# Router rows of 4 in 26 edge columns picked by one-hot products in place of gathers, and each expert's weights asked for one expert ahead

## The chip, the core and the metric

The kernel runs on one core of one Trainium2 chip. The core has five engines, each with its own queue of instructions that it works through in order: TensorE (PE: matmuls; its weight loads are a row of their own, PEld), VectorE (DVE), ScalarE (ACT), GpSimd (POOL) and SyncE (SP, which here does nothing but issue DMAs). They wait for one another through semaphores. Sixteen DMA engines move data between DRAM and the on-chip memory SBUF; matmuls write to a second on-chip memory, PSUM. A gather by a list of row numbers (an indirect DMA) is issued from POOL, one instruction for 128 rows; plain DMAs are issued from SP.

The metric is the device time of one execution in microseconds, as a median over runs. Lower is better.

## The reference, cut to what matters

The model has a graph network over 103,125 edges, a linear-attention transformer of depth 4 beside it, and then a mixture of four experts whose router is itself a graph attention over 65,536 edges. The change lies in this last part. The reference of the router and the experts, with nodes x (3,125 rows of 256):

```python
h = (x_flat @ W_gat).reshape(M, HEADS, NUM_EXPERTS)
src = jnp.concatenate([edge_index[0], loops])
dst = jnp.concatenate([edge_index[1], loops])
a_src = (h * att_src).sum(-1)
a_dst = (h * att_dst).sum(-1)
e = leaky_relu(a_src[src] + a_dst[dst], negative_slope=0.2)
e_max = segment_max(e, dst, num_segments=M)
ee = jnp.exp(e - e_max[dst])
denom = segment_sum(ee, dst, num_segments=M)
alpha = ee / (denom[dst] + 1e-16)
msg = h[src] * alpha[:, :, None]
agg = segment_sum(msg, dst, num_segments=M).reshape(M, HEADS * NUM_EXPERTS) + b_gat
scores = layernorm(agg, ln_gamma, ln_beta).reshape(M, HEADS, NUM_EXPERTS).mean(1)
topk_s, topk_i = jax.lax.top_k(scores, TOP_K)
w = jax.nn.softmax(topk_s, axis=-1)
for ei in range(NUM_EXPERTS):
    g = jnp.where(topk_i == ei, w, 0.0).sum(-1)
    hh = gelu(x @ W1[ei] + b1[ei])
    out = out + g[..., None] * (hh @ W2[ei] + b2[ei])
```

What has to be fetched per edge is the source node's row: 16 values of h and 4 of a_src. The experts' products do not depend on the router; only the weights g with which they are added at the end do.

## The kernel before

**What comes first.** Up to about 1,900 us the kernel does the graph network and the transformer and, beside them, sorts the router's edges by their target node. The sort ends in a table in DRAM, `by_dst`, which holds the source node of each edge in sorted order; `sorted_edges` (L925) reads it back as the tile `si`, 128 partitions by 512 columns of node numbers. Only the first FEW = 400 columns hold edges here; columns from 400 on are worked only when a flag, `many`, is set (L1410), which it is not with these inputs. `finish` (L832) makes for every chunk of four node tiles the normed rows `hT`, the router's row of each node in `tab` (16 values of h, 4 of a_src, 4 of a_dst) and stores `tab` to DRAM as `tab_d` (L863).

**The stage of the change.** The 400 columns are cut into 16 chunks: 15 of 26 columns and a last one of 10 (`COLS`, L1247; `N_FEW` is 16).

- `gathered(j)` (L1255) takes one of three buffers `rows_c` and fills it for chunk j: one gather on POOL for each column, which fetches for 128 edges the rows of `tab_d` named by `si`.
- `edge_chunk(j, ...)` (L1272) works chunk j on DVE: it loads the targets' part `tg` from DRAM, adds source and target parts into `ev` (L1300, the first to read the rows), takes a running maximum by scans, and has ACT take two exponentials (`exp`, L1274, pinned to its place in ACT's order). It then multiplies the rows by the exponentials (L1315), runs 20 scans over them (L1321) and stores the chunk to DRAM (L1322). Each chunk carries on from the chunk before.
- `expert(e)` (L1342) is a generator: it loads an expert's weights (`we1`, `we2`, `be1`, each with a single buffer) and then yields seven pieces of work. A piece takes four tiles of 128 nodes (the last piece one): eight matmuls of 512 columns into three PSUM buffers `ps_a` (L1353), a Gelu on ACT for each of four results (L1355), then 16 matmuls of 256 columns and a bias product into `ps_t` (L1361, L1364) and a copy by ACT into `y_all` (L1367).

**The order.** The loop at L1382 sets it. For chunk j the program first asks for the gathers of chunk j + 1, then lays out the expert pieces up to (j + 1.5) x 1.75 of the 28, and then the edge chunk j. The last piece is kept for after the last chunk. The framework's planner may put an instruction ahead of earlier ones of its engine when those are not ready by its own reckoning; among ready ones the program's order counts. On the chip each engine's order is then fixed.

**What follows.** `fetch_sums` gathers 25 columns of finished sums, `over_partitions` joins the partitions' ends, `gates` makes the weights g, and `by_diagonals` and `by_turns` add up the experts' outputs and store the result.

**Buffers that the change borrows.** In the pool `so`, tiles with the same tag share a ring of buffers. The tags "hr" and "earlier" (two buffers each of 2 KB per partition), "oh_lo" (three), "oh_hi" and "run" (two), "pairs" and "place" (one each) belong to the edge sort, which is over when the stage begins; `si` itself sits in one of the "oh_hi" buffers. The tail uses "pairs" again for `sums`, "hr" for `more`, "earlier" for `ag` and `ag2`, and "oh_lo" for the small tiles of `across`.

Of the kernel before, what the change touches and what calls it, by code (L numbers as in the profile page):

```python
# [8 lines left out]
F32 = mybir.dt.float32  # L9
BF16 = mybir.dt.bfloat16  # L10
I32 = mybir.dt.int32
F16 = mybir.dt.float16
AF = mybir.ActivationFunctionType
ALU = mybir.AluOpType
AX = mybir.AxisListType
# [3 lines left out]
P = 128  # L19
N = 3125  # L20
NT = 25
NP = NT * P
LAST = N - (NT - 1) * P
D = 256
# [17 lines left out]
NEXP = 4  # L42
# [7 lines left out]
FEW = 400  # L50
NONE = NT * P - 1
FF2 = 512
# [7 lines left out]
def kernel(ctx: ExitStack, tc: tile.TileContext, a: dict, out: bass.AP):  # L60
    nc = tc.nc
    ctx.enter_context(nc.allow_non_contiguous_dma(reason="short vectors by partition"))
    V, S, G, T = nc.vector, nc.scalar, nc.gpsimd, nc.tensor
# [4 lines left out]
    dram = ctx.enter_context(tc.tile_pool(name="dram", bufs=1, space=DRAM))  # L68
    pg = ctx.enter_context(tc.tile_pool(name="pg", bufs=2, space=PSUM))
    pa = ctx.enter_context(tc.tile_pool(name="pa", bufs=3, space=PSUM))  # L70
    pt = ctx.enter_context(tc.tile_pool(name="pt", bufs=2, space=PSUM))
# [3 lines left out]
    ident = const.tile([P, P], F32, name="ident")  # L75
# [6 lines left out]
                    base=0, channel_multiplier=-1)  # L82
    after = const.tile([P, P], F32, name="after")
    G.affine_select(out=after, in_=ones, pattern=[[-1, P]], compare_op=ALU.is_gt, fill=0.0,
                    base=0, channel_multiplier=1)
# [45 lines left out]
    def by_column(pool, vec, c, name):  # L131
        t = pool.tile([P, c], F32, name=name)
        nc.sync.dma_start(t, vec.rearrange("(c p) -> p c", p=P))
        return t

    def weight(pool, w, c, n, name):
        t = pool.tile([P, c, n], F32, name=name)
        nc.sync.dma_start(t, w.rearrange("(c p) n -> p c n", p=P))
        return t
# [36 lines left out]
    hT = state.tile([P, 2, NP], F32, name="hT")  # L176
    tab = state.tile([P, NT, ROW + 1], F32, name="tab")
# [3 lines left out]
    so = ctx.enter_context(tc.tile_pool(name="so", bufs=1))  # L181
# [54 lines left out]
    ps = pg.tile([P, DM], F32, name="ps_g")  # L236
# [11 lines left out]
    e, e_src = (so.tile([P, TE], I32, name=f"e_{k}", tag="hr", bufs=2) for k in range(2))  # L248
# [95 lines left out]
    ps = pt.tile([P, 512], F32, name="ps_t")  # L344
# [11 lines left out]
    bin_p = const.tile([P, 1], F32, name="bin_p")  # L356
# [314 lines left out]
    place = so.tile([P, TE], I32, name="place")  # L671
# [259 lines left out]
    NCH = HG + H4  # L931
# [307 lines left out]
    ex = ctx.enter_context(tc.tile_pool(name="ex", bufs=1))  # L1239
# [3 lines left out]
    def gtile(shape, name, dt=F32, **k):  # L1243
        return ga_pool.tile(shape, dt, name=name, **k)

    CW = 28
    COLS = list(range(0, FEW, 26)) + list(range(FEW, TE, CW)) + [TE]  # L1247
# [4 lines left out]
    tgt_p = tgt_d[:E2, :].rearrange("(p t) h -> p t h", t=TE)  # L1252
    si = edges["si"]

    def gathered(j):  # L1255
        rows_c = gtile([P, CW, ROW], "rows_c", bufs=3)
        for t in range(COLS[j], COLS[j + 1]):
            G.indirect_dma_start(out=rows_c[:, t - COLS[j], :], out_offset=None, in_=tab_d,  # L1258
                                     in_offset=bass.IndirectOffsetOnAxis(ap=si[:, t:t + 1], axis=0))
        return rows_c  # L1260


# [70 lines left out]
    def y_of(e, t):  # L1333
# [5 lines left out]
            return hT[:, :, c0:c0 + P]  # L1339
        return hT[:, i // 2, c0 + i % 2 * D:c0 + i % 2 * D + D]  # L1340

    def expert(e):  # L1342
        we1 = weight(ex, a["L0_ffn_W1"][e], 2, FF2, "we1")
        we2 = weight(ex, a["L0_ffn_W2"][e], FF2 // P, D, "we2")
        be1 = by_column(ex, a["L0_ffn_b1"][e], FF2 // P, "be1")
        be2 = be2s[e]
        for c in FOURS:
            w = len(c) * P
            hh = []
            for f in range(FF2 // P):  # L1350
                ps = pa.tile([P, 512], F32, name="ps_a")
                for kc in range(2):
                    T.matmul(ps[:, :w], we1[:, kc, f * P:(f + 1) * P], hT[:, kc, c[0] * P:c[0] * P + w], start=kc == 0, stop=kc == 1)  # L1353
                hf = ex.tile([P, 512], F32, name="hf", bufs=5)
                S.activation(hf[:, :w], ps[:, :w], AF.Gelu, bias=be1[:, f:f + 1])  # L1355
                hh.append(hf)
            for i0 in range(0, len(c), 2):
                ts = c[i0:i0 + 2]
                k = len(ts)
                ps = pt.tile([P, 2, D], F32, name="ps_t")  # L1360
                T.matmul(ps[:, :k, :], ones_b, be2[:, :k, :], start=True, stop=False, skip_group_check=True)  # L1361
                for i in range(k):
                    for f in range(FF2 // P):
                        T.matmul(ps[:, i, :], hh[f][:, (i0 + i) * P:(i0 + i + 1) * P], we2[:, f, :],  # L1364
                                 start=False, stop=f == FF2 // P - 1, skip_group_check=True)
                if e < NEXP - 1:
                    S.copy(y_all[:, e, ts[0]:ts[-1] + 1, :], ps[:, :k, :])  # L1367
                elif k == 2:
                    S.copy(hT[:, i0 // 2, c[0] * P:c[0] * P + 2 * D], ps.rearrange("p t d -> p (t d)"))
                else:  # L1370
                    S.copy(hT[:, :, c[0] * P:c[0] * P + P], ps[:, 0, :].rearrange("p (a d) -> p a d", a=2))
            yield True

    be2s = [bias_rows(so, a["L0_ffn_b2"][e], f"be2{e}", tags) for e, tags in enumerate((
        ("own_bin", "lo", "base"), ("own_bin", "hi", "base"), ("own_bin", "ohT1", "base"), ("own_bin", "ohT0", "base")))]
    work = (w for e in range(NEXP) for w in expert(e))
    PIECES = NEXP * len(FOURS)
    EACH = PIECES / N_FEW
    done = 0
    last, taken = None, gathered(0)  # L1380
    many = nc.values_load(many_i[0:1, 0:1], min_val=0, max_val=1)
    for j in range(N_FEW):  # L1382
        rows_j = taken
        if j + 1 < N_FEW:
            taken = gathered(j + 1)

        while done < min((j + 1.5) * EACH, PIECES - 1) and next(work, False):
            done += 1
        last = edge_chunk(j, rows_j, last, j == N_FEW - 1)
        if j == 0:  # L1390
            V.tensor_scalar(flag0, flag0, -1.0, 1.0, op0=ALU.mult, op1=ALU.add)
            V.tensor_tensor(goes, f0[:, 0:1], f0[:, 1:2], op=ALU.is_equal)
            V.tensor_tensor(goes, goes, flag0[:, 1:2], op=ALU.mult)
            V.tensor_tensor(whole, goes, flag0[:, 0:1], op=ALU.mult)
            V.tensor_tensor(ends_in, flag0[:, 0:1], whole, op=ALU.subtract)
            V.tensor_scalar(whole_r, whole, -1.0, BIG, op0=ALU.add, op1=ALU.mult)
            V.tensor_scalar(own_row[:, 0:1], f0[:, 0:1], 0.0, float(NP - 1), op0=ALU.max, op1=ALU.min)
            V.tensor_single_scalar(own_row[:, 1:2], own_row[:, 0:1], 7, op=ALU.logical_shift_right)
            V.tensor_single_scalar(own_row[:, 0:1], own_row[:, 0:1], P - 1, op=ALU.bitwise_and)
            V.tensor_scalar(goes, bin_p, float(NP), None, op0=ALU.add)  # L1400
            V.scalar_tensor_tensor(flag0[:, 0:1], own_row[:, 0:1], float(NT), own_row[:, 1:2], op0=ALU.mult, op1=ALU.add)
            V.tensor_tensor(flag0[:, 0:1], flag0[:, 0:1], goes, op=ALU.subtract)
            V.scalar_tensor_tensor(carry_to, flag0[:, 0:1], ends_in, goes, op0=ALU.mult, op1=ALU.add)
            V.tensor_scalar(kept, ones, whole_r, None, op0=ALU.mult)
            ps = pg.tile([P, P], F32, name="ps_g")
            T.transpose(ps, kept, ident)
            V.tensor_copy(kept[:32, :], ps[:32, :])
    for _ in work:
        pass
    with tc.If(many > 0):  # L1410
        last = {"m": end_m, "ad": end_ad, "rows": end_rows}
        for j in range(N_FEW, len(COLS) - 1):
            last = edge_chunk(j, gathered(j), last, j == len(COLS) - 2)
# [193 lines left out]
    for _ in gates(1):  # L1607
        for _ in range(1):
            if len(laid_out) < 3:
                c = by_pe[len(laid_out)]  # L1610
                laid_out.append((c, by_diagonals(c)))
    n_laid = len(laid_out)
    for k, c in enumerate(by_pe):
        added(*laid_out[k])
        if n_laid < len(by_pe):
            c = by_pe[n_laid]
# [28 lines left out]
```

## Time and profile before

| what | value |
|---|---|
| median of 3 runs | 2523.63 us (2521.66 to 2525.22) |
| the profiled execution | 2525.02 us, span 2523.3 us |
| mean granted TensorE clock | 0.891 |
| PE busy | 1996.1 us (79% of the span) |
| DVE busy | 1397.8 us (55%) |
| ACT busy | 1169.1 us (46%) |
| POOL busy | 1791.2 us (71%) |
| first gather of `rows_c` issued | 1932.9 us |
| last gather of `rows_c` issued | 2441.6 us |
| in 1933 to 2443: PE, DVE, ACT, POOL busy | 367.3, 120.6, 142.3, 387.9 us |

How to read it: "busy" is the sum of an engine's instruction times as the hardware profiler recorded them; the time between two instructions is put down to whatever released the second ("issue" where nothing that the profile shows did). In the list of groups, a row gives source line, engine, operation, output and input tiles, count, then busy us and mean ns of one, then the idle time just before the group's instructions and what ended most of it. The slices cut the span into 40 equal parts of 63 us and give the busy share in tenths.

### The profile page before, as it was taken

Reading aid. Unit: us, or ns where it says so; the run is one execution under the profiler, and the core shown is the slowest. Engines: PE = TensorE matmul, PEld = TensorE weight load, DVE = VectorE, ACT = ScalarE, POOL = GpSimd, SP = SyncE. Lnnn points to the kernel's source line nnn. Section 1 sums busy time; section 2 is a strip of 40 time slices with the busy share of each in tenths; the row PEclk is TensorE's granted clock in tenths of the full one; section 3 lists DMA queues with packets and bytes.
Section 4 is the critical chain, followed back from the end, with each engine's and each line's share of the span. In section 5 each row is a group of like instructions: output and inputs, shape, how many; then the busy total and the mean of one; then the engine's idle time right before and its main releaser. Section 6 shows DMA issues by size and latency. Waiting matters only on the chain. (4 is left out here: it accounts for less than half of the span.)

```text
span 2523.3 us, 31735 instructions
## 1 busy us (share of the span) xinstructions
PE 1996.1 (79%) x9924; PEld 1392.4 (55%) x9924; DVE 1397.8 (55%) x4366; ACT 1169.1 (46%) x2039; POOL 1791.2 (71%) x1814
## 2 busy tenths in 40 slices
PE   3869778487779988879499989899999859485934
PEld 2656555365556666556266666666767535353624
DVE  7886876677777668677154444664531222222246
ACT  5656555345345445445254665665453223232314
POOL 4675767667767777767777777777777777777762
PEclk9979888698989998989799989999999879797967
DMA  8976778878878887878311112222100111112112
GB/s 252 317 248 215 249 208 269 204 254 278 288 251 270 270 266 256 276 251 270 83 38 30 40 42 70 63 56 57 32 17 14 22 39 22 34 23 38 22 21 60
DMA packets 301856, 360.53 MB, mean 143 GB/s; under 512 B 183905, under 2 KB 248826, under 8 KB 288474
## 3 DMA queue, kind: packets, MB, share of 16 engines
q1 hardware_dynamic: 230762, 242.78, 30.2%
q0 software_dynamic: 70912, 115.59, 17.0%
q8 instruction: 81, 1.33, 0.2%
q14 instruction: 101, 0.83, 0.1%
HBM read 202.22 MB, written 160.09 MB: 144 GB/s over the span
## 5 line engine op out<-in xcount | busy, mean ns | idle before, releaser
L515 POOL DMA_INDIRECT m_run<-xn_d,src_i x806 | 818.3, 1015 | 372.7 <-issue 214.5
L805 POOL DMA_INDIRECT by_dst<-pairs,place x512 | 504.1, 985 | 156.1 <-issue 153.3
L527 DVE SCALAR_TENSOR_TENSOR m_run<-m_run,stay 128x320 f32<-128x320 f32 x805 | 439.1, 545 | 89.8 <-DMA m_run<-xn_d,src_i 78.3
L1258 POOL DMA_INDIRECT rows_c<-tab_d,si x400 | 388.1, 970 | 121.9 <-issue 120.4
L1149 PE MATMUL ps_a<-h,w 128*128 128x512 f32 (+1 forms) x896 | 389.6, 580 | 6.1 <-ACT h L165 6.0
L1160 PE MATMUL ps_a<-w,gT 128*128 128x256 f32 x1600 | 365.1, 383 | 0.0
L1160 PEld LDWEIGHTS ps_a<-w,gT 128*128 128x128 f32 x1600 | 303.9, 192 | 49.0 <-issue 7.1
L1353 PE MATMUL ps_a<-hT,we 128*128 128x512 f32 (+1 forms) x448 | 199.6, 597 | 139.1 <-ACT hf L1355 75.5
L1149 PEld LDWEIGHTS ps_a<-h,w 128*128 128x128 f32 x896 | 165.3, 203 | 166.6 <-issue 147.3
L1300 DVE TENSOR_TENSOR ev<-ad,rows_c 128x104 f32<-128x104 f32 (+1 forms) x16 | 6.2, 391 | 385.6 <-DMA rows_c<-tab_d,si 380.7
L1353 PEld LDWEIGHTS ps_a<-hT,we 128*128 128x128 f32 x448 | 85.5, 205 | 233.5 <-ACT hf L1355 85.1
L1150 ACT ACTIVATE gT<-ps_a,b 128x512 f32<-128x512 f32 (+1 forms) x224 | 140.5, 637 | 136.8 <-PE ps_a L1149 135.5
L1364 PE MATMUL ps_t<-we,hf 128*128 128x256 f32 x800 | 184.9, 385 | 0.0
L1364 PEld LDWEIGHTS ps_t<-we,hf 128*128 128x128 f32 x800 | 155.3, 195 | 33.4 <-issue 10.4
L124 ACT ACTIVATE hn<-xm,rstd 128x256 f32<-128x256 f32 x225 | 120.9, 594 | 56.2 <-DVE rstd L120 52.1
L776 ACT ACTIVATE earlier<-ps_t,slope 128x512 f16<-128x512 f32 x128 | 93.8, 773 | 114.6 <-PE ps_t L775 112.8
L160 PE MATMUL ps_t<-ident,hn 128*128 128x128 f32 x450 | 83.3, 316 | 48.3 <-ACT hn L124 44.6
L1087 PE MATMUL ps_g<-xm,kr 128*128 128x256 f32 x400 | 108.8, 410 | 8.6 <-ACT kr L1085 8.2
L1061 PE MATMUL ps_a<-wq,h 128*128 128x256 f32 x400 | 100.4, 394 | 18.1 <-ACT kT L1041 11.8
L1029 PE MATMUL ps_a<-h,wk 128*128 128x512 f32 (+1 forms) x224 | 100.7, 583 | 2.7 <-ACT h L165 2.7
L160 PEld LDWEIGHTS ps_t<-ident,hn 128*128 128x128 f32 x450 | 56.6, 157 | 82.9 <-ACT hn L124 64.0
L1355 ACT ACTIVATE hf<-ps_a,be 128x512 f32<-128x512 f32 (+1 forms) x112 | 69.0, 641 | 70.8 <-PE ps_a L1353 69.9
(418 smaller groups left out, 3391.6 us busy)
## 6 DMA issues: line engine op xcount, KB each, us to landing
run_d<-m_run SPq DMA_DIRECT2D x100, 1280.0 KB
m_run<-in_edge_attr_dram SPq DMA_DIRECT2D x95, 256.0 KB
hr<-row_h SPq DMA_DIRECT2D x64, 256.0 KB
m_run<-xn_d,src_i POOLq DMA_INDIRECT x806
w<-in_L_mix_W_dram SPq DMA_DIRECT2D x8, 1024.0 KB
by_dst<-pairs,place POOLq DMA_INDIRECT x512
rows_c<-tab_d,si POOLq DMA_INDIRECT x400
run_d<-rows_c SPq DMA_DIRECT2D x15, 312.0 KB
```

Source lines behind the costliest of these rows:

```text
L124: S.activation(dst, src, AF.Identity, bias=r[:, 1, i:i + 1], scale=r[:, 0, i:i + 1])
L160: T.transpose(ps[:, i * P:(i + 1) * P], src[:, c * P:(c + 1) * P], ident)
L515: last_gather[0] = G.indirect_dma_start(out=m[:, t, :D], out_offset=None, in_=xn_d, in_offset=bass.IndirectOffsetOnAxis(ap=src_i[:, t0 + t ...
L527: add = V.scalar_tensor_tensor(m[:, t, :], before_m, stay[:, c:c + 1], m[:, t, :], op0=ALU.mult, op1=ALU.add)
L805: i = G.indirect_dma_start(out=by_dst, out_offset=bass.IndirectOffsetOnAxis(ap=place[:, t:t + 1], axis=0), in_=pairs0[:, t:t + 1], in_offs ...
L1087: T.matmul(ps_x[:, m, :], kr[:, m * P:(m + 1) * P], xm[:, t, :], start=i == 0 and m == 0, stop=i == len(c) - 1, skip_group_check=True)
L1149: T.matmul(ps[:, :w], ff_w[l]["w1"][:, kc, f * P:(f + 1) * P], h2[:, kc, :w], start=kc == 0, stop=kc == 1)
L1150: S.activation(gT[:, f, :w], ps[:, :w], AF.Gelu, bias=ff_w[l]["b1"][:, f:f + 1])
L1160: T.matmul(ps[:, i, :], gT[:, f, (2 * i0 + i) * P:(2 * i0 + i + 1) * P], ff_w[l]["w2"][:, f, :], start=False, stop=f == FF // P - 1, skip_ ...
L1258: G.indirect_dma_start(out=rows_c[:, t - COLS[j], :], out_offset=None, in_=tab_d, in_offset=bass.IndirectOffsetOnAxis(ap=si[:, t:t + 1], a ...
L1353: T.matmul(ps[:, :w], we1[:, kc, f * P:(f + 1) * P], hT[:, kc, c[0] * P:c[0] * P + w], start=kc == 0, stop=kc == 1)
L1364: T.matmul(ps[:, i, :], hh[f][:, (i0 + i) * P:(i0 + i + 1) * P], we2[:, f, :], start=False, stop=f == FF2 // P - 1, skip_group_check=True)
```

## The change

**Part one.** In each of the first 15 chunks the gathers fetch 22 of the 26 columns. The other four columns are made by `by_products(j, rows_c)`, called at the end of `gathered(j)`. The node number of an edge is split into low seven bits and the rest. The low parts of the 60 columns are transposed, stored to DRAM as 16-bit floats (`low_d`) and read back per chunk, broadcast to all partitions (`low_rows`). A compare with the partition's own number gives one-hot columns `which`. A matmul with the whole table of nodes (`tab_c`, 25 tiles by 20 values = 500 columns) picks, for each of 128 edges, the rows of all 25 nodes with that low part. DVE then compares the tile number with the edge's high part (`high_of`), multiplies the product by the result in place, and sums over the 25 tiles into `rows_c`. The setup ahead of the loop splits the numbers, makes `tab_c`, and has POOL write the tile numbers.

**Part two.** `expert_weights(e)` replaces the loads at the head of `expert`. The weights of expert 0 are loaded as before; those of expert e + 1 are asked for at the end of the second piece of expert e. Even experts use the buffers `we1` and `we2`; odd ones use two buffers each under the tags "hr" and "earlier", in halves.

```diff
+    PER, BY_PE = 26, 4
+    N_PE = FEW // PER
+    picked = si[:, :N_PE * PER].rearrange("p (j w) -> p j w", w=PER)[:, :, PER - BY_PE:]
+    part_i = so.tile([P, N_PE, BY_PE], I32, name="part_i", tag="oh_lo", bufs=3)
+    high_of = so.tile([P, N_PE * BY_PE], F32, name="high_of", tag="run", bufs=2)
+    V.tensor_single_scalar(part_i, picked, 7, op=ALU.logical_shift_right)
+    V.tensor_copy(high_of, part_i.rearrange("p j w -> p (j w)"))
+    V.tensor_single_scalar(part_i, picked, P - 1, op=ALU.bitwise_and)
+    low_of = so.tile([P, N_PE * BY_PE], F32, name="low_of", tag="oh_lo", bufs=3)
+    V.tensor_copy(low_of, part_i.rearrange("p j w -> p (j w)"))
+    ps = pt.tile([P, 512], F32, name="ps_t")
+    T.transpose(ps[:N_PE * BY_PE, :P], low_of, ident)
+    low_t = so.tile([P, P], F16, name="low_t", tag="oh_lo", bufs=3)
+    S.copy(low_t[:N_PE * BY_PE, :], ps[:N_PE * BY_PE, :P])
+    low_d = dram.tile([N_PE, BY_PE * P], F16, name="low_d")
+    nc.sync.dma_start(low_d.rearrange("j (w e) -> (j w) e", w=BY_PE), low_t[:N_PE * BY_PE, :])
+    low_rows = so.tile([P, BY_PE * P], F16, name="low_rows", tag="oh_hi", bufs=2)
+    which = so.tile([P, BY_PE * P], F32, name="which", tag="pairs")
+    tab_c = so.tile([P, NT, NCH], F32, name="tab_c", tag="place")
+    V.tensor_copy(tab_c, tab[:, :, :NCH])
+    tile_ids = so.tile([P, NT], F32, name="tile_ids", tag="run", bufs=2)
+    G.iota(tile_ids, pattern=[[1, NT]], base=0, channel_multiplier=0, allow_small_or_imprecise_dtypes=True)
+
+    def by_products(j, rows_c):
+        nc.sync.dma_start(low_rows, low_d[j:j + 1, :].to_broadcast([P, BY_PE * P]))
+        V.tensor_scalar(which, low_rows, bin_p, None, op0=ALU.is_equal)
+        for k in range(BY_PE):
+            ps = pg.tile([P, NT, NCH], F32, name="ps_g")
+            T.matmul(ps, which[:, k * P:(k + 1) * P], tab_c, start=True, stop=True)
+            V.scalar_tensor_tensor(ps, tile_ids.rearrange("p (t o) -> p t o", o=1).to_broadcast([P, NT, NCH]),
+                                   high_of[:, j * BY_PE + k:j * BY_PE + k + 1], ps, op0=ALU.is_equal, op1=ALU.mult)
+            V.tensor_reduce(rows_c[:, PER - BY_PE + k, :NCH], ps.rearrange("p t f -> p f t"), AX.X, ALU.add)
+
     def gathered(j):
         rows_c = gtile([P, CW, ROW], "rows_c", bufs=3)
-        for t in range(COLS[j], COLS[j + 1]):
+        for t in range(COLS[j], COLS[j] + PER - BY_PE if j < N_PE else COLS[j + 1]):
             G.indirect_dma_start(out=rows_c[:, t - COLS[j], :], out_offset=None, in_=tab_d,
                                      in_offset=bass.IndirectOffsetOnAxis(ap=si[:, t:t + 1], axis=0))
+        if j < N_PE:
+            by_products(j, rows_c)
         return rows_c
...
+    def expert_weights(e):
+        be1 = ex.tile([P, FF2 // P], F32, name="be1", bufs=2)
+        nc.sync.dma_start(be1, a["L0_ffn_b1"][e].rearrange("(c p) -> p c", p=P))
+        if e % 2 == 0:
+            we1 = weight(ex, a["L0_ffn_W1"][e], 2, FF2, "we1")
+            we2 = weight(ex, a["L0_ffn_W2"][e], FF2 // P, D, "we2")
+            return [we1[:, k, :] for k in range(2)], [we2[:, f, :] for f in range(FF2 // P)], be1
+        w1, w2 = [], []
+        for k in range(2):
+            t = so.tile([P, FF2], F32, name="we1h", tag="hr", bufs=2)
+            nc.sync.dma_start(t, a["L0_ffn_W1"][e][k * P:(k + 1) * P, :])
+            w1.append(t)
+        for k in range(2):
+            t = so.tile([P, 2, D], F32, name="we2h", tag="earlier", bufs=2)
+            nc.sync.dma_start(t, a["L0_ffn_W2"][e][2 * k * P:2 * (k + 1) * P, :].rearrange("(c p) n -> p c n", p=P))
+            w2 += [t[:, i, :] for i in range(2)]
+        return w1, w2, be1
+
+    loaded = []
+
     def expert(e):
-        we1 = weight(ex, a["L0_ffn_W1"][e], 2, FF2, "we1")
-        we2 = weight(ex, a["L0_ffn_W2"][e], FF2 // P, D, "we2")
-        be1 = by_column(ex, a["L0_ffn_b1"][e], FF2 // P, "be1")
+        if e == 0:
+            loaded.append(expert_weights(0))
+        we1, we2, be1 = loaded.pop()
...
+            if c[0] == 4 and e + 1 < NEXP:
+                loaded.append(expert_weights(e + 1))
             yield True
```

The matmuls of an expert read the same weights through lists of slices (`we1[kc]`, `we2[f]`).

More of the change, by code (lines that the diff above doesn't have):

```diff
@@ L1352, in expert @@
                 for kc in range(2):
-                    T.matmul(ps[:, :w], we1[:, kc, f * P:(f + 1) * P], hT[:, kc, c[0] * P:c[0] * P + w], start=kc == 0, stop=kc == 1)
+                    T.matmul(ps[:, :w], we1[kc][:, f * P:(f + 1) * P], hT[:, kc, c[0] * P:c[0] * P + w], start=kc == 0, stop=kc == 1)
                 hf = ex.tile([P, 512], F32, name="hf", bufs=5)
@@ L1363, in expert @@
                     for f in range(FF2 // P):
-                        T.matmul(ps[:, i, :], hh[f][:, (i0 + i) * P:(i0 + i + 1) * P], we2[:, f, :],
+                        T.matmul(ps[:, i, :], hh[f][:, (i0 + i) * P:(i0 + i + 1) * P], we2[f],
                                  start=False, stop=f == FF2 // P - 1, skip_group_check=True)
```

## The prediction

> **What bounds the kernel now.** I read the slices of the page first, then the cost groups, then who waits for whom, then the timelines of POOL, PE and DVE over the stage that the diff touches.
>
> ```profile
> PE   3869778487779988879499989899999859485934
> POOL 4675767667767777767777777777777777777762
> DMA  8976778878878887878311112222100111112112
> ...
> L1258 POOL DMA_INDIRECT rows_c<-tab_d,si x400 | 388.1, 970 | 121.9 <-issue 120.4
> L1353 PE MATMUL ps_a<-hT,we 128*128 128x512 f32 (+1 forms) x448 | 199.6, 597 | 139.1 <-ACT hf L1355 75.5
> L1300 DVE TENSOR_TENSOR ev<-ad,rows_c 128x104 f32<-128x104 f32 (+1 forms) x16 | 6.2, 391 | 385.6 <-DMA rows_c<-tab_d,si 380.7
> ```
>
> One slice is 63 us. From slice 31 on POOL stays at its 7 (it never shows more, because 0.30 us lie between any two of its DMAs), while PE falls to 4 or 5 every second slice and the DMA engines stand at 1 or 2. The 400 gathers take 388.1 + 121.9 = 510.0 us, and the waiting in them is "issue", so POOL waits for nobody. DVE, the reader of the rows, idles 380.7 us for them. The answer on waits, cut to the stage (us in total, times, longest), says the same from the other side:
>
> ```profile
> DVE ev L1300 <- DMA rows_c<-tab_d,si: 380.7, 15, 28.6
> ACT ev L1275 <- DVE ev L1306: 124.0, 16, 17.3
> ...
> PE ps_a L1353 <- ACT hf L1355: 75.5, 12, 20.3
> ...
> PE ps_a L1353 <- DMA we<-in_L_ffn_W_dram: 63.6, 3, 22.6
> ```
>
> PE's 63.6 us for weights and its 75.5 us for ACT are real, but not on the path: ACT stands at the chunk's exp for 124.0 us because the rows have not come. The POOL timeline gives the step:
>
> ```profile
> 1979.94 0.94 POOL L1258 DMA_INDIRECT rows_c<-tab_d,si  x1 [0.30 <-issue]
> 1981.19 0.94 POOL L1258 DMA_INDIRECT rows_c<-tab_d,si  x1 [0.30 <-issue]
> ```
>
> 1981.19 - 1979.94 = 1.25 us per column (1.2475 over longer stretches). The gathers run from 1932.9 to 2442.6; then come 81 us of tail (the two-part gates, the sums, the output) that the diff leaves alone.
>
> **Part one: 60 gathers leave POOL.** FEW // 26 = 15 chunks lose 4 columns each. 60 x 1.2475 = **-74.9 us**. By the average over the stage, 510 / 400 = 1.275, it would be 76.5; the difference is one 4.28 us gather and some stretched ones, which need not go in proportion, so I take 74.9. Next late behind POOL would be PE (below). Added on POOL is one iota of 25 columns: the rows of that shape (L878, L402) have 0.15 us.
>
> **What it adds on PE.** A product is 128x128 by 128x500 in f32. L1353's calls of 512 columns are two instructions each (448 for 224 calls), and 16 of them take 7.03 us in a steady stretch, so 0.44 us each and 0.88 a call; for 500 columns 0.86 us. 60 x 0.86 = 52 us. The experts themselves: a full piece is 14.2 us (1983.34 to 1997.55), the 128-row piece 3.6, so 4 x (6 x 14.2 + 3.6) = 355 us. Together 407 us of PE against 340 x 1.2475 = 424 us of POOL, and PE starts its first piece at 1913, 20 us before POOL. PE has cover, but thin: 25.7 us per chunk (14.2 x 24/16 + 3.6 x 4/16 + 3.4) beside POOL's 22 x 1.2475 = 27.4.
>
> **What it adds on DVE.** Per column a compare-multiply and a reduce over 500 values of PSUM. Nearest rows: L1067, PSUM with a broadcast, 128x512, 683 ns; L1094, the same operation on PSUM, 128x256, 469 against 410 for a plain add. So 0.67 to 0.75 us, taken 0.70. The reduce: L1030, 512 of PSUM read in order, 689 ns; this one strides, and L1552 (240 values, strided, 574 ns) against L1542 (in order, 406 ns) is a factor of 1.4, so 0.67 to 0.95, taken 0.85. Per chunk also one compare of 512 (L341's 419 ns). Sum: 60 x 1.55 + 15 x 0.42 + setup 2 = 101 us beside the stage's 121 busy us of 510; DVE idles 380 us, so nothing, as long as its order is not what blocks (rival B).
>
> **Setup.** si is issued on SP at 1926.75, behind the last tab_d write. Small DMAs come back in about 2.5 us here (flags, issued 1934.74, used 1937.26). So: si 1929.3, four DVE operations 0.8, transpose and ACT copy 1.0, low_d out 2.5, low_rows in 2.5, compare 0.4: first product at about 1936.5. The first chunk's gathers are over at 1960 even with 22 columns, so the edge chunk loses nothing; PE may stand some 10 us, since the products come before the first piece in program order. SP gets 16 small DMAs and 4 more weight parts, 0.45 us each: 9 us over a stage in which it mostly waits. In that queue the row loads stand between the tg loads and the stores of finished chunks; each waits for one compare at most, and rows_c's three buffers give POOL over a chunk of slack.
>
> **A rule that speaks against it.** Row first: all 400 gathers together are 388.1 - 400 x 0.944 = 10.5 us over their usual 0.944, 3.3 of it in one of them, so 7.2 us beside 121 us of DVE, copies and tensor_scalars among them. The Trainium skill, page "SBUF — State Buffer", section "Who interferes with whom", says that a DVE copy or tensor_scalar in a two-port mode locks GpSimd out for the whole instruction. By the rule the 15 compares and the setup copies cost POOL 15 x 0.42 + 2 = 8 us; by the row 101 us of new DVE work cost at most 7.2 x 101 / 121 = 6, and the same page excepts a reduce, and any operation with one SBUF input outside these modes, which is most of that work. I take **+3 us**, ends 0 and 8.
>
> **Part two: weights one expert ahead.** It takes PE's three stops of 63.6 us. By itself, beside 510 us of gathers, it is worth 0 (cover: POOL). Beside 424 us it is needed: 407 + 64 would not fit. The load is asked for after the second of an expert's seven pieces, some 65 us ahead of its use, and the stops show that a load lands within 23 us; its buffers were last used by the expert two before, or by edge sorting that is over. On SP the three or five loads move ahead of some five tg loads and stores, which wait 0.45 us more for each; a store has two chunks' time.
>
> **Sum.** -74.9 + 0.15 + 3 = -71.7. Profiled execution: 2525.0 (span 2523.3 and 1.7 around it) - 71.7 = 2453; the median of 2523.63, 1.4 lower, gives **2452 us**.
>
> **Where the queues couple.** New is that PE waits for DVE inside each chunk. Two PSUM buffers serve four products, so the third waits for the first reduce, and behind it PE's queue holds the expert pieces, behind which ACT's exp for this chunk stands. Let s be PE's stop per chunk beyond its work. Without POOL in the way, PE reaches the exp of chunk 14 at 1913 + 404 + 10 (setup) + 15 s; POOL has its rows at 1932.9 + 330 x 1.2475 + 2 = 2347. (404 is 407 without the last short piece.) So s costs nothing up to 20 / 15 = 1.3 us, and at 1.3 + 71.7 / 15 = 6.1 us it has eaten the whole gain. If the pick-ups go ahead of the chunk's scans on DVE, or other matmuls stand between the second and third product, s is near 0 whenever PE is the late one. If all four products stand together and DVE does its scans first, then: exp 1.9 us after the piece (copy 0.58, table load 1.28), 0.6 for both exps, 4.2 of scans, 1.55 + 0.86 and 1.55 on, so PE resumes at 10.8 instead of 3.4: s = 7.4. Pieces come 2, 2, 2 (one short) and 1 to a chunk, so PE is late by up to some 10 us within four chunks and back in time at their end; three row buffers cover that. I take s below 1.3, because the present PE timeline shows other ready matmuls put between dependent ones (L853 among L1353).
>
> **Rivals.**
> - A, PE becomes the bound, still faster (chance 0.18): s near 3, or weights that arrive late because SP holds them back (the change not doing what it says: +64 on PE). Ends at 2452 + 15 x 3 - 20 = 2477, with late weights 2452 + 64 - 20 = 2496. For it: the thin cover. Against: PE's stops now are waits for the rows and the weights, and both shrink.
> - B, the coupling at full price (0.09): s = 7.4 gives 2452 + 111 - 20 = **2543**, slower; it decides from 6.1 on. For it: the scans come earlier in program order than the next products' pick-up. Against: ACT's table load and exps leave DVE a gap of over 2 us just then.
> - C, no change (0.02): s by chance between 5.8 and 6.4, 2524.
> - Main case 0.71: 2446 to 2460.
>
> **The numbers.** What a measurement of this kernel can tell from no change is about 0.2%, 5 us. Faster is main and A, 0.89; same 0.02; slower 0.09. The range runs from 2444 (no contention, -76.5, and 0.1%) to 2492, which leaves out B, C and A's upper end.
>
> **What would show it.** Gathers x340, mean still 0.95 to 1.0 us, their stretch near 427 us and the tail behind them near 81. PE waiting for the weights: gone. ACT's wait at the exp well below 124 us but not near 0; near 0 means that PE is the bound (A). DVE's wait for rows_c near 200 us (427 less 220 busy); if instead PE waits for ps_g's readers by over 20 us in total and POOL for rows_c's buffers, the coupling (A, B) has it. POOL gathers at a mean over 1.0 would speak for the lock rule. The prediction is wrong if the gathers end before 2372 and the tail starts late all the same.

## The result, and the profile after

The changed kernel takes **2497.31 us** in the median (2494.52 to 2499.97, 4 runs) beside 2524.43 for the kernel before on the same chip: ratio 0.9893, 95% interval 0.9876 to 0.9911. It is faster, by 27 us and not by the 72 that were forecast, and the time lies above the upper end of the range, 2492. The profiled execution has a span of 2498.3 us.

First the page's slices and three of its groups:

```profile
PE   3869778587879998879499988899999698888874
POOL 4575667667767777766777777777776766666652
...
L1291 POOL DMA_INDIRECT rows_c<-tab_d,si x340 | 326.7, 961 | 150.2 <-issue 100.4
...
L1284 DVE SCALAR_TENSOR_TENSOR ps_g<-tile_ids,high_of,ps_g 128x500 f32<-128x500 f32 x60 | 43.8, 740 | 169.4 <-PE ps_g L1283 168.3
...
L1283 PE MATMUL ps_g<-tab_c,which 128*128 128x500 f32 x120 | 69.0, 700 | 67.0 <-DVE rows_c L1286 64.3
```

PE's holes of every second slice are filled (after a 6 in slice 32, 8 and 9 to slice 38), and POOL, which had stood at 7 to the end, now shows sixes. The 60 gathers are gone, yet "issue" is no longer all of POOL's waiting: 150.2 - 100.4 leaves 50 us that it spent on somebody. The first gather is issued at 1939.8 and the last at 2415.3, a stretch of 476 us where 427 was forecast. The tail behind it hardly moved: 83 us from the last issue to the end, where it was 82.

Who held it is in the answer on waits (us in total, times, longest):

```profile
PE ps_g L1283 <- DVE rows_c L1286: 64.3, 13, 14.5
DVE ev L1335 <- DMA rows_c<-tab_d,si: 59.4, 8, 14.8
POOL rows_c L1291 <- DVE rows_c L1356: 48.8, 7, 8.9
```

Three engines wait for each other. PE's product waits for a pick-up (the reduce L1286); DVE waits for gathered rows (380.7 us before); POOL waits for DVE's scans (L1356), which hold the row buffer it wants to fill. PE's stops for weights and ACT's stop at the exponential are gone from the list. One turn of the timeline (start, duration, instruction, idle before and its releaser) shows how the three hang together:

```profile
2029.58 3.92 DVE L1356 TENSOR_TENSOR_SCAN rows_c<-mr,rows_c 128x26 f32<-128x26 f32 x20
...
2033.77 0.94 POOL L1291 DMA_INDIRECT rows_c<-tab_d,si  x1 [8.88 <-DVE rows_c L1356]
...
2060.25 0.94 POOL L1291 DMA_INDIRECT rows_c<-tab_d,si  x1 [0.30 <-issue]
...
2062.75 0.43 DVE L1335 TENSOR_TENSOR ev<-ad,rows_c 128x104 f32<-128x104 f32 x1 [7.38 <-DMA rows_c<-tab_d,si]
2063.10 1.25 DVE L1286 TENSOR_REDUCE rows_c<-ps_g 128x20 f32<-128x500 f32 x2
2063.82 3.70 PE L1283 MATMUL ps_g<-tab_c,which 128*128 128x500 f32 x4 [7.92 <-DVE rows_c L1286]
```

The scans end at 2033.50 and let POOL start a chunk at 2033.77. Its 22nd gather goes out at 2060.25. DVE's first read of those rows, L1335, waits for them until 2062.75, and only after it come the two reduces, in DVE's queue. They free PSUM for the third product, so PE stands for 7.92 us until 2063.82, with the experts' matmuls behind it in its own queue. Those matmuls feed ACT, ACT's exponential stands behind its Gelus, DVE's next scans need the exponential, and POOL's next buffer needs the scans. In the order in which DVE was built, a chunk is: two compare-multiplies of chunk j+1; the rest and the scans of chunk j-1; the read L1335 of chunk j; then the two reduces of chunk j+1 and its other pick-ups. That is the theory (T): **pick-ups that need no gather stand behind an instruction that waits for gathers.** The buffer is late for one more reason: a chunk's scans begin from the last row of the chunk before, inside its row buffer, so that buffer is in use for one chunk longer.

The rivals: R1, PE is simply full here, busy for 406 of these 476 us (the 417 us of the expectations below are those of 1933 to 2440); R2, DVE's added work slows POOL's gathers.

### The profile page after: what moved, and what is told of

Its sections match the earlier page's. It is cut to its first block, busy times and chain, and to the rows that moved or that the text cites. A ratio compares the mean times of both kernels' runs of the same rounds, so it can differ in the third digit from the quotient of the medians.

```text
span 2498.3 us, 32120 instructions
## 1 busy us (share of the span) xinstructions
PE 2047.1 (82%) x10045; PEld 1417.0 (57%) x10045; DVE 1481.2 (59%) x4506; ACT 1168.8 (47%) x2040; POOL 1723.6 (69%) x1755
## 5 line engine op out<-in xcount | busy, mean ns | idle before, releaser
L1291 POOL DMA_INDIRECT rows_c<-tab_d,si x340 | 326.7, 961 | 150.2 <-issue 100.4
L1284 DVE SCALAR_TENSOR_TENSOR ps_g<-tile_ids,high_of,ps_g 128x500 f32<-128x500 f32 x60 | 43.8, 740 | 169.4 <-PE ps_g L1283 168.3
L1283 PE MATMUL ps_g<-tab_c,which 128*128 128x500 f32 x120 | 69.0, 700 | 67.0 <-DVE rows_c L1286 64.3
L1087 PEld LDWEIGHTS ps_g<-xm,kr 128*128 128x128 f32 x400 | 78.6, 205 | 44.2 <-ACT kr L1085 29.0
L1138 PE MATMUL ps_a<-co,hT 128*128 128x256 f32 x400 | 99.3, 391 | 0.8 <-DVE co L1129 0.6
L718 ACT CAST counts<-ps_g 128x256 f16<-128x256 f32 x64 | 80.3, 1375 | 41.5 <-PE ps_g L716 21.4
```

What stands on the lines that cost most here:

```text
L1087: T.matmul(ps_x[:, m, :], kr[:, m * P:(m + 1) * P], xm[:, t, :], start=i == 0 and m == 0, stop=i == len(c) - 1, skip_group_check=True)
```

## The experiments

### A first series

It ran on a chip on which the kernel before took 3655 us; the changed kernel itself has no run there. The edits of the first three are shown below, where they were run again; the fourth is the diff without part two.

> Edit: in the changed kernel, the first read of chunk j's gathered rows on DVE (ev) is ordered behind the last pick-up of chunk j+1's four products; three row buffers stay. Theory (PE's queue hangs on a DVE read that waits for the gathers): in the changed kernel the pick-ups of products one and two stand behind ev, so the third product and all expert matmuls behind it wait for gathers of the chunk before. With this order PE's stops at the products (64 us) go to under 10, POOL's wait for row buffers (49 us) to under 15, the gathers' stretch from 476 to 427-440 us, time 2452 to 2466. Rival R1 (PE's own work, 417 us plus table loads, is the bound): time stays within 10 us of 2497 and PE has no gap to give. Rival R2 (DVE's new work slows POOL's descriptor writing): the stretch stays at 476 and the gathers' mean stays.

> Edit: in the changed kernel, the last row of each chunk is copied to a small tile after the scans, and the next chunk's scans start from the copy; so a row buffer is free once its chunk is stored, not only after the next chunk's scans. No order is forced. Theory: POOL's wait for row buffers goes to 0-5 us; three of four pick-ups can be planned ahead of ev because their buffer is free, so PE's stops at the products fall from 64 us to under 25; time 2452 to 2470. R1: within 10 us of 2497. R2: stretch and mean of the gathers unchanged.

> Edit: both edits of the two runs before together. Theory: POOL never waits, stretch 340 x 1.2475 + at most 10 = 424 to 434 us, time 2448 to 2460. R1: within 10 us of 2497. R2: stretch unchanged.

> Edit: only the first part of the change; each expert's weights are loaded at its head as before, into single buffers. Theory: three stops of about 21 us return on PE, which is now on the path at least half of the time; time 2515 to 2560. R2 (POOL slowed by DVE): no difference from 2497. If weights never mattered beside the coupling, 2497 to 2505.

Measured, as ratios to the kernel before: 0.9995 (0.9964 to 1.0025), 0.9888 (0.9803 to 0.9973), 1.0047 (1.0019 to 1.0075) and 0.9988 (0.9960 to 1.0016). Here the order shows no gain, alone or with the last row apart, and the last row alone gains 1.1%. The timeline of the first run, 2,750 us ahead of the stage in question, shows why they decide nothing:

```profile
110.77 0.69 DVE L1066 TENSOR_REDUCE qm<-ps_a 128x16 f32<-128x512 f32 x1 [6.75 <-remote]
110.77 1.44 ACT L165 ACTIVATE h<-ps_t,b1n,g 128x512 f32<-128x512 f32 x2 [9.36 <-remote]
110.90 0.94 POOL L515 DMA_INDIRECT m_run<-xn_d,src_i  x1 [0.30 <-issue]
...
111.60 0.69 PE L1083 MATMUL ps_t<-ident,kT 128*128 128x128 f32 x2 [9.26 <-issue]
```

DVE, ACT and PE stand still for 7 to 9 us and start again together, released by nothing that the profile names, while POOL goes on at its step of 1.25 us. Such stops run through the whole span; a gather's median is 944 ns there too. Where all three compute engines are held back like this, POOL is not what ends the stage (in the first run it waits 256 us for row buffers), and sparing it gathers or waits moves little. T, R1 and R2 were tried again where the kernel before takes 2526 us.

### Is it the order, the buffer, or PE?

The changed kernel itself ran beside three versions of it. In the second, an order on DVE alone: chunk j's first read comes behind the last pick-up of chunk j+1.

```diff
     def by_products(j, rows_c):
...
-            V.tensor_reduce(rows_c[:, PER - BY_PE + k, :NCH], ps.rearrange("p t f -> p f t"), AX.X, ALU.add)
+            picked_up.append(V.tensor_reduce(rows_c[:, PER - BY_PE + k, :NCH], ps.rearrange("p t f -> p f t"), AX.X, ALU.add))
...
+        if j + 1 < N_PE:
+            tc.add_manual_dep(landed.ins, picked_up[-1].ins.name, later, reason="the next chunk's products are picked up first")
```

In the third, the last row is copied out, so that the row buffer comes free one chunk earlier. The fourth has both.

```diff
-        at = {"m": m[:, :, w], "ad": ad[:, :, w - 1], "rows": rows_c[:, w - 1, :NCH], "summed": summed}
+        last_row = gtile([P, NCH], "last_row")
+        V.tensor_copy(last_row, rows_c[:, w - 1, :NCH])
+        at = {"m": m[:, :, w], "ad": ad[:, :, w - 1], "rows": last_row, "summed": summed}
```

> The changed kernel itself, beside the kernel before and the three versions that follow, on one chip. It sets the base for them: 2485 to 2510 us where the kernel before takes 2510 to 2535, ratio 0.988 to 0.991. If the ratio comes out at 0.995 or above, the chip holds the compute engines back by something that no theory here is about, and then the three versions cannot be told apart by their times either; the rows to compare are then only the waits of the 15 chunks.

> One order changed: VectorE picks up all four products of chunk j+1 before it does the step on chunk j (L1335 of the changed kernel) that waits for chunk j's gathers. Theory T (the wait for gathers stands in front of two pick-ups, and so in front of TensorE): TensorE's waits for a pick-up fall from 64 us to under 25, VectorE's wait for gathers stays or grows since it is nobody's bound, 2455 to 2475 us, ratio to before 0.973 to 0.981. But the pick-ups still write a row buffer that the scans of chunk j-1 hold, so GpSimd's waits for row buffers (49 us) may stay: then 2475 to 2490. Rival R1 (TensorE is full in this stretch, 417 us of work and not the order): 2490 to 2505. Rival R2 (VectorE's added work slows GpSimd's gathers): the gathers' stretch stays at 470 to 480 us, 2490 to 2505.

> The last row of a chunk is copied to a small tile, so its row buffer is free one chunk earlier; 16 small copies are added on VectorE, some 4 us, beside other work. VectorE's order is left to the planner, which then can place pick-ups earlier. Theory T (the row buffer is held over one chunk too long, which sets both the late pick-ups and GpSimd's waits): GpSimd's waits for rows fall from 49 us to under 15, TensorE's waits for a pick-up to under 30, stretch 435 to 450 us, 2460 to 2475 us. R1: 2490 to 2505, waits moved and not gone. R2: same.

> Both at once: the last row apart, and all four pick-ups of chunk j+1 ahead of the first read of chunk j's gathers. Theory T: the loop is open on both sides, GpSimd runs its 340 gathers at 1.26 us each, 428 us and a few, stretch 430 to 442 us, 2450 to 2465 us, ratio 0.971 to 0.977. If it is no better than the better of the two single versions, one of the two holds was enough, or a third wait has come in. R1: 2490 to 2505. R2: gathers' mean duration above 1.0 us or the stretch at 470.

| version | us, median | ratio to before (95%) | gathers, first to last issued | PE waits for pick-ups | POOL waits for rows |
|---|---|---|---|---|---|
| before | 2526.12 | | 509 | | 0 |
| changed kernel | 2490.04 | 0.9860 (0.9841 to 0.9879) | 476 | 61.2 | 50.4 |
| order only | 2449.75 | 0.9698 (0.9681 to 0.9714) | 430 | 13.9 | none |
| last row apart | 2451.31 | 0.9698 (0.9675 to 0.9722) | 433 | 19.1 | 0.3 |
| both | 2455.02 | 0.9709 (0.9675 to 0.9744) | 430 | 17.8 | none |

(The stretch of the kernel before is from its one profile.) One order on DVE, with no work taken away, is worth 40 us. R1 falls: PE has the same work, and the stage is through in 430 us. R2 falls: the pick-ups are all still there. T holds, and more strongly than expected: the order alone also clears POOL's waits, and the order and the last row each end below their bands (2455 to 2475 and 2460 to 2475), and both together inside theirs. The changed kernel's time is in its band, its ratio a little under (0.988 to 0.991). The waits of the order-only kernel:

```profile
DVE ev L1337 <- DMA rows_c<-tab_d,si: 131.3, 16, 12.5
POOL rows_c L1293 <- issue: 100.8, 331, 0.3
...
PE ps_g L1285 <- DVE rows_c L1288: 13.9, 12, 4.3
```

Now DVE waits more for the rows (131 us where it was 59), which is where waiting belongs while POOL is the bound, and POOL waits for nobody. Its timeline:

```profile
2028.89 1.26 DVE L1288 TENSOR_REDUCE rows_c<-ps_g 128x20 f32<-128x500 f32 x2
2029.63 1.94 PE L1285 MATMUL ps_g<-tab_c,which 128*128 128x500 f32 x4 [0.23 <-DVE rows_c L1288]
...
2033.18 0.67 DVE L1288 TENSOR_REDUCE rows_c<-ps_g 128x20 f32<-128x500 f32 x1
...
2045.07 0.40 DVE L1337 TENSOR_TENSOR ev<-ad,rows_c 128x104 f32<-128x104 f32 x1 [11.21 <-DMA rows_c<-tab_d,si]
```

All four pick-ups are over by 2033.85, 11 us before the read that waits for gathers; PE stands 0.23 us and not 7.92. With the last row apart the planner by itself put reduces ahead of the read, so either cut opens the loop and the second adds nothing: the three versions' intervals overlap.

### What are the weights worth?

Part two alone (the diff without by_products and with all 400 gathers), then part one alone, then part one with the order above. In the last two, expert begins as in the kernel before:

```diff
-        if e == 0:
-            loaded.append(expert_weights(0))
-        we1, we2, be1 = loaded.pop()
+        we1 = weight(ex, a["L0_ffn_W1"][e], 2, FF2, "we1")
+        we2 = weight(ex, a["L0_ffn_W2"][e], FF2 // P, D, "we2")
+        be1 = by_column(ex, a["L0_ffn_b1"][e], FF2 // P, "be1")
...
-            if c[0] == 4 and e + 1 < NEXP:
-                loaded.append(expert_weights(e + 1))
```

> The second part of the change alone: all 400 gathers as before, an expert's weights loaded one expert ahead. GpSimd's 400 gathers at 1.25 us each end the stretch and TensorE's stops for weights lie beside them, so the time stays: ratio 0.997 to 1.003 of the kernel before, with TensorE's wait for weights (64 us before) gone from the trace. If TensorE's stops did count somewhere, it is faster by more than that.

> The first part alone, order left to the planner, an expert's weights loaded when the expert begins, as before. Theory T: the wait of TensorE for pick-ups behind gathers stays (64 us in the changed kernel) and the waits for weights (64 us before) come on top where the two do not meet: 2510 to 2550 us, ratio 0.994 to 1.010. If the two waits meet, 2495 to 2510. If the weights' stops had been hidden for another reason, as fast as the changed kernel, 2490.

> The first part with the four pick-ups of chunk j+1 ordered ahead of the step that waits for chunk j's gathers (2450 us with both parts), and the weights as before. It prices the second part where GpSimd is held back by nothing else. TensorE has 417 us of work in the stretch and 64 us of waits for weights, 481 against GpSimd's 430: 2485 to 2505 us, ratio 0.984 to 0.992. If the weights part is worth nothing even here, 2450, ratio 0.970.

Beside 2525.60 us for the kernel before: weights alone 2524.47, ratio 0.9999 (0.9988 to 1.0010), as expected. Products alone 2495.21, 0.9878 (0.9860 to 0.9896); products with the order 2449.01, 0.9692 (0.9674 to 0.9710). These two are as fast as with part two (0.9860 to 0.9893, and 0.9698), against the main expectation of both: **the weights part is worth nothing even where PE has no time to spare.** Where PE's stops of before came from is in SP's timeline of before, beside DVE's and PE's:

```profile
2018.02 1.95 PE L1353 MATMUL ps_a<-hT,we 128*128 128x128 f32 x16
...
2035.29 0.40 DVE L1300 TENSOR_TENSOR ev<-ad,rows_c 128x104 f32<-128x104 f32 x1 [24.74 <-DMA rows_c<-tab_d,si]
...
2038.70 0.32 SPq L1279 DMA_DIRECT2D tg<-tgt_d  x1
2039.07 0.44 SPq L138 DMA_DIRECT2D we<-in_L_ffn_W_dram  x1
...
2043.12 3.78 PE L1353 MATMUL ps_a<-hT,we 128*128 128x512 f32 x4 [20.48 <-DMA we<-in_L_ffn_W_dram]
```

PE's last use of the old first-layer weights is over at 2019.97. The new ones could be asked for then, but at the head of SP's queue stands a tg load of the edge chunk, which waits for DVE, which waits for gathers until 2035.29. SP's own waits of before, over 1935 to 2400, say how long such loads stand:

```profile
SPq L1279 <- DVE rows_c L1315: 341.5, 12, 31.8
```

The load goes out at 2039.07, when PE has stood for 16.4 of its 20.48 us. So most of the stop named "weights" was a wait for POOL. The other two stops are alike: their loads go out at 2171.13 and 2302.87, each 0.41 us after a tg load. With the products PE no longer runs ahead of the chunks, and in the products-with-order kernel the same place reads:

```profile
2031.94 0.39 SPq L138 DMA_DIRECT2D we<-in_L_ffn_W_dram  x1
...
2033.59 1.84 PE L1285 MATMUL ps_g<-tab_c,which 128*128 128x500 f32 x4
2035.64 6.28 PE L1392 MATMUL ps_a<-hT,we 128*128 128x512 f32 x14 [0.22 <-DMA we<-in_L_ffn_W_dram]
```

tg has gone out a microsecond earlier (2030.91), the load follows PE's last use at once, lands in under 4 us behind a bias product, eight matmuls and two products, and PE waits 0.22 us. In the weights-only kernel the 63.6 us did not become time either: PE's wait for ACT's hf grows from 75.5 to 140.1 us.

```profile
PE ps_a L1373 <- ACT hf L1375: 140.1, 15, 20.0
```

### A fifth column

The order version with BY_PE = 5; two small tiles (high_of, kept) change their buffers so that it fits.

```diff
-    PER, BY_PE = 26, 4
+    PER, BY_PE = 26, 5
...
-    high_of = so.tile([P, N_PE * BY_PE], F32, name="high_of", tag="run", bufs=2)
+    high_of = so.tile([P, N_PE * BY_PE], F32, name="high_of", tag="oh_lo", bufs=3)
...
-    kept = gtile([P, P], "kept")
+    kept = so.tile([P, P], F32, name="kept", tag="run", bufs=2)
```

> The best version with 5 of 26 columns by products (325 gathers, 75 products). GpSimd's sum is 325 x 1.264 = 411 us where 340 took 430; TensorE's is 417 + 15 x 0.86 = 430 and its short waits. If TensorE is the next bound close behind: 2440 to 2460 us, ratio 0.966 to 0.974, no gain on 4 columns. If GpSimd still ends the stretch: 2428 to 2436, ratio 0.961 to 0.965. If the pick-ups on VectorE (15 x 1.41 us more) come late: above 2460.

2435.28 us (2430.75 to 2437.38), ratio 0.9646 (0.9630 to 0.9662): the fastest version, 14 us below the products-with-order kernel of the same series, whose four runs do not overlap with these. It falls in the band where POOL ends the stretch, but not cleanly. The busy times in 1940 to 2340 (PE, PEld, DVE, ACT, POOL, then granted clock, DMA share and GB/s):

```profile
1940.00:2340.00 400.00, 397.15 (x1353) 246.35 (x1352) 219.28 (x768) 135.10 (x207) 299.22 (x310) 1.00 0.19 34
```

PE is busy for 397 of 400 us, and POOL begins to wait for row buffers again (7.5 us). The gathers go from 1928.6 to 2346.3, 418 us for 325, or 1.285 each where the four-column version has 430 / 340 = 1.265. PE and POOL are level here; a sixth column was not tried.

## Why the prediction was right and wrong

- **Gathers, -74.9 us, and contention, +3.** Right where the loop is open: the order-only kernel is 76.4 us below before, 2452 was forecast and 2449.75 measured. Contention was too high: 340 gathers at 1.2475 are 424, so the 431 us from first issue to last end hold 7 us of extra, and before had 510 - 499 = 11. So the two-port rule of the Trainium skill (page "SBUF — State Buffer", section "Who interferes with whom"), priced at 8 us, shows nothing here: in the order-only kernel DVE is busy 89 us longer and a gather's mean is 964 ns where it was 970. Of the 14 gathers that run beside a compare (L1282) for over 0.2 us, 13 take 940 to 947 ns and one 1,192. Whether the compares ran in such a mode, no run shows.
- **PE's 52 us for 60 products.** About right: PE's busy time grows from 1996.1 to 2047.1 in this profile, and by 36 to 44 us in the six later profiles of kernels with four columns beside 2526 us. **DVE's 1.55 us per column** was 0.74 + 0.67 = 1.41; the strided reduce takes no more than the 689 ns of the in-order one that it was scaled from, so the factor of 1.4 was not needed.
- **Setup.** First product at 1946.7, forecast 1936.5; 7 of the 10 us are the list si arriving later, with the whole stage. The start of the gathers lies between 1924.6 and 1941.6 in the profiles of the products kernels, so such a shift is not the change's doing.
- **Weights: nothing by itself** was right. **"Beside 424 us it is needed: 407 + 64 would not fit"** is a wrong step, though it cost the forecast nothing: the 64 us were read as a load that is asked for too late, and were for the most part SP's queue held by a tg load that waits for POOL.
- **The step that failed is s**, PE's stop per chunk: "I take s below 1.3, because the present PE timeline shows other ready matmuls put between dependent ones". Measured it is 64.3 / 15 = **4.3 us**. Put into the prediction's own sum for rival A, 2452 + 15 x 4.3 - 20 = 2496, and 2497 was measured. The sum holds elsewhere too: 61.2 us of stops give 2493 where 2490 was measured, and the 13.9 us of the order-only kernel, under the 20 that cost nothing, give 2452 where 2450 was measured. The mechanism had been named; its size was wrong. Two things were missing. The worst case was laid out with the chunk's scans in front of the pick-ups (7.4 us), but not with the read of the rows in front of them, which waits for POOL itself; the first such stop is 14.5 us, and six of about 7.9 us make up nearly all the rest. And "three row buffers cover that", which also stood under Setup as "over a chunk of slack", is wrong, since the scans of chunk j-1 still read chunk j-2's last row and so hold the buffer that chunk j+1 is to fill.
- **The signs named beforehand worked.** PE waiting for ps_g's readers by over 20 us (64.3) together with POOL for row buffers (48.8), and ACT's wait at the exponential near 0, were to mean A or B, and did. The chances did not: A had 0.18, and its upper end was left out of the range. Two sums are off by 0.1 us, without effect: the worst case's 10.8 adds up to 10.7, and the 25.7 per chunk to 25.6; the plain add of 128x256 from PSUM (L646) has 417 ns and not 410.

## What to carry to other kernels

When work is moved from a bound engine to others, write down the fixed order of every queue it enters and look for an instruction in front of it that waits for the engine just relieved: that closes a loop, and part of the gain goes round in it. A buffer is in use until its last reader, which can be the next iteration's start value, so count slack from there. A wait that the trace puts down to a load is worth its length only if the load was issued when it could be; look first at what stood before it in the issuing queue.

## What the runs showed of the hardware

The halts of the first series were not expected: stops of PE, ACT and DVE together, the longest of 23 us (616.8 to 640.2 in the first run, while POOL starts 17 gathers), and 3655 us for a kernel that elsewhere takes 2526; the profile names no cause, and it stays open. The granted clock in a stretch goes with how full PE is: in 1940 to 2340 it is 0.86 before (PE busy 286 of 400 us), 0.92 in the changed kernel (333), 0.97 with the order (382) and 1.00 with five columns (397). Matmuls of one kind hardly show it: the 800 of the experts' second product have a median of 379 ns in each of these kernels, and a mean of 385 before, 381 in the changed kernel, 383 with the order and 380 with five columns. That is some 5 us at most, so a low figure there is here a sign of gaps more than a cause of the time.
